# Attention stage of a two-layer metaformer: keys of two heads in one row tile, projections and transposes put into other rounds, LayerNorm statistics behind the reciprocal

## The chip, the cores and the metric

The kernel runs on one core of one Trainium2 chip, as one program in one launch. The metric is the device time in microseconds (us), the median of several runs. Engines are named as in the profile: PE is TensorE's matmul, PEld its weight load, DVE is VectorE, ACT is ScalarE, POOL is GpSimd and SP is the engine that issues most of the DMAs. L604 is line 604 of the kernel before; the change shortens the file, so the same work has a slightly lower number after it (L604 becomes L598, for instance).

## The reference

The reference is a network of two layers on x of shape 8 x 128 x 32 x 32, with a normalisation and a residual around each part. The change touches the first part alone, which is an attention over heads and, for each query row, over the keys of one image row:

```python
xp = jnp.transpose(x, (0, 2, 3, 1))                 # x is already normalised over channels
q = (xp @ wq.T).reshape(b, h, w, n, d)              # n = 8 heads of d = 16
k = (xp @ wk.T).reshape(b, h, w, n, d)
v = (xp @ wv.T).reshape(b, h, w, n, d)
weights = jnp.einsum('bhwnd,bxynd->bnhwxy', q, k) * scale
weights = jax.nn.softmax(weights, axis=-1)          # over y, 32 keys at a time
attn = jnp.einsum('bnhwxy,bxynd->bhwnd', weights, v)
out = attn.reshape(b, h, w, c)
...
x = x + _L0_conv_ref(_ln_c(x), L0_conv_wq, L0_conv_wk, L0_conv_wv)
```

The softmax runs over groups of 32 keys, so each query has 32 separate sums for a head. The rest of the network (a spectral mixer, a deformable convolution, a mixture of experts) is not touched. All arithmetic is in float32.

## The kernel before, in words

A small test at the start decides between a general attention and `attention_bounded`, which leaves out the row maximum; with these inputs the second runs, and the profile shows it from 32 us to about 890 us. Everything below is about it.

**Rounds.** The work is written out by hand as a list of rounds. There are 8 images of 32 rounds each. An image has 8 units of four rounds: a unit is a block of 256 queries (`qc`) and a group of four heads (`hg`). A call `at(round, order, do, ...)` puts a step into a round; the list is sorted by round and by order, and each engine then runs its instructions in that sequence, without overtaking.

**What a round does.** In each round `scores` (L604) computes one PSUM tile of 4 heads x 2 key tiles x 256 queries on PE, in eight matmuls of 32 contraction rows, four side by side in the array. ACT takes the exponential of the tile (L609). The PSUM tile `s` has one buffer of four banks, so the scores of the next round wait until the exponential has read it. POOL adds the two key tiles (`add_tiles`, L618). With a unit starting at round t0, the rest follows later: the sums `z` (L625, PE) in round t0+5, the reciprocals (L632, DVE) behind them, `spread_out` (L639, PE) in t0+6, `divide` (L646, DVE) in t0+6 to t0+9, and `values` (L656, PE) in t0+8 to t0+11. Since every t0 is a multiple of four, PE's regular work depends on the round modulo 4: in round 0 the values of one and a half tiles, in round 1 half a tile and `z`, in round 2 a tile and `spread_out`, in round 3 a tile. Every eight rounds, in round 0 modulo 8, `results` (L673) brings a finished block back to rows of tokens by a matmul with the 0/1 matrix `pick`, ACT copies it, and POOL adds it to the residual (L681).

**What an image needs beside its rounds.** Before its first round an image must be loaded and transposed to tokens (`tokens`, L539), normalised (`layer_norm_pieces`, L79 to L105), transposed back (`channels`, L547, into the tile `hk`), and projected: `keys` (L573), `queries` (L559) and `key_values` (L585). All of these share one PSUM bank, `small_bank`, with `z` and `results`; ACT empties it. The normalisation is 25 pieces: eight statistics on DVE (two instructions each, L79 and L80), nine pieces of an inverse square root by Newton steps on POOL (17 instructions of 128 x 8 elements, L87 to L99), and eight `norm` pieces on ACT (L105), which read the last result `nm` of the POOL pieces. The rounds in which all this stands are lists relative to `first`, the image's first round:

```python
project_at = [first + n for n in (-13, -12, -9, -5, -4, -1, 3, 4, 7, 11)]
turn = {"channels": (first - 20, first - 17)}
...
turn.update(load=first - 42, tokens=(first - 38, first - 34))
norm_at = [first - n for n in (
    37, 36, 35, 34, 33, 32, 32, 31, *range(31, 22, -1), 22, 22, 22, 21, 19, 19, 18, 18
)]
```

**Keys and queries.** Heads of 16 channels are padded to row tiles of 32. Head group `hg` has heads 4 hg to 4 hg + 3, one in each row tile, with zeros in the upper 16 rows of both `wq` and `wk`; so an image has four projections of keys (two head groups x two halves), four of queries and two of values.

Of the kernel before, what the change touches and what calls it, by code (L numbers as in the profile page):

```python
# [399 lines left out]
class BoundedAttention:  # L400
# [6 lines left out]
    def __init__(self, nc, cp):  # L407
        self.nc = nc
        HG, NH = self.HG, self.NH
        self.xc = cp.tile([P, T], F32, name="xc")  # L410
        self.ht = cp.tile([P, NT, C], F32, name="ht")
        self.hk = cp.tile([P, T], F32, name="hk")
        self.wq, self.wk = (cp.tile([P, HG, NH, 32], F32, name=n) for n in ("wq", "wk"))
        self.wv = cp.tile([C, C], F32, name="wv")
        self.group = cp.tile([P, NG], F32, name="group")
        self.spread = cp.tile([P, 2, P], F32, name="spread")
        self.pick = cp.tile([P, HG, NH, HD], F32, name="pick")

    def keys_view(self):
        return self.hk.rearrange("c (r p) -> c r p", p=P)  # L420

    def tokens(self, x, ident, pool, ps):

        nc = self.nc
        nc.sync.dma_start(self.xc, x[0].rearrange("c h w -> c (h w)"))
        xv = self.xc.rearrange("c (i p two) -> c two i p", two=2, p=P)
        st = pool.tile([P, NT, 6], F32, name="f_st")
        mv = pool.tile([P, NT, 2], F32, name="f_mv")
        banks = []
        for par in range(2):  # L430
            pt = ps.tile([P, 4, P], F32, tag="x", name="p_x")
            for i in range(4):
                nc.tensor.transpose(pt[:, i, :], xv[:, par, i, :], ident)
            banks.append(pt)
            for i in range(4):
                nc.vector.bn_stats(st[:, 4 * par + i, :], pt[:, i, :])
                nc.vector.bn_aggr(mv[:, 4 * par + i, :], st[:, 4 * par + i, :])
        rs = inverse_std(nc, pool, mv[:, :, 1], 1e-6, nc.vector)
        for par in range(2):
            for i in range(4):  # L440
                n = 4 * par + i
                nc.vector.tensor_scalar(
                    self.ht[:, n, :], banks[par][:, i, :], mv[:, n, 0:1], rs[:, n : n + 1],
                    ALU.subtract, ALU.mult,
                )
# [3 lines left out]
            nc.scalar.copy(  # L449
                self.keys_view()[:, 4 * par : 4 * par + 4, :].rearrange(  # L450
                    "c r (g m) -> c r g m", m=4
                ),
                pb.rearrange("c i p -> c (i p)").rearrange("c (g r m) -> c r g m", r=4, m=4),
            )

    def matrices(self, wqT, wkT, wvT):
        nc, HG, NH = self.nc, self.HG, self.NH
        for w, src in ((self.wk, wkT), (self.wq, wqT)):
            nc.gpsimd.memset(w, 0.0)
            for hg in range(HG):  # L460
                nc.sync.dma_start(
                    w[:, hg, :, 0:HD],
                    src[:, hg * NH * HD : (hg + 1) * NH * HD].rearrange("c (h d) -> c h d", d=HD),
                )
        nc.sync.dma_start(self.wv, wvT)

        group = self.group
        nc.gpsimd.memset(group, 1.0)
        nc.gpsimd.affine_select(
            out=group, in_=group, pattern=[[-4, NG]], base=0, channel_multiplier=1,  # L470
            compare_op=ALU.is_ge, fill=0.0,
        )
        nc.gpsimd.affine_select(
            out=group, in_=group, pattern=[[4, NG]], base=3, channel_multiplier=-1,
            compare_op=ALU.is_ge, fill=0.0,
        )

# [9 lines left out]
        nc.gpsimd.memset(self.pick, 0.0)  # L487
        for hg in range(HG):
            nc.gpsimd.affine_select(
                out=self.pick[:, hg], in_=self.pick[:, hg], pattern=[[-32, NH], [-1, HD]],  # L490
                base=-HD * hg, channel_multiplier=1, compare_op=ALU.not_equal, fill=1.0,
            )


def attention_bounded(ctx, tc, ident, x, x1d, given, weigh, head):


# [8 lines left out]
    QU = 256  # L506
    QC = T // QU
    UNITS = HG * QC
    wq, wk, wv = given.wq, given.wk, given.wv
    group, spread, pick = given.group, given.spread, given.pick  # L510
    hk = given.keys_view()
# [31 lines left out]
    def channels(par):  # L543
# [6 lines left out]
        nc.scalar.copy(  # L550
            hk[:, 4 * par : 4 * par + 4, :].rearrange("c r (g m) -> c r g m", m=4),
            pt.rearrange("c (g r m) -> c r g m", r=4, m=4),
        )

    def queries(img, hg, par):
# [3 lines left out]
        nc.tensor.matmul(  # L559
            pq, wq[:, hg].rearrange("c h d -> c (h d)"),  # L560
            hk[:, 4 * par : 4 * par + 4, :].rearrange("c r p -> c (r p)"),
            start=True, stop=True,
        )
        nc.scalar.copy(
# [1 line left out]
            pq.rearrange("p (r g m) -> p r g m", r=4, m=4),  # L566
        )

    def keys(img, hg, par):
        if "k" not in img:  # L570
            img["k"] = sb.tile([P, HG, NT, P], F32, tag="k", name="k")
        pk = small_bank("pk")
        nc.tensor.matmul(  # L573
            pk, wk[:, hg].rearrange("c h d -> c (h d)"),
            hk[:, 4 * par : 4 * par + 4, :].rearrange("c r p -> c (r p)"),
            start=True, stop=True,
        )
        nc.scalar.copy(
            img["k"][:, hg, 4 * par : 4 * par + 4, :].rearrange("p c n -> p (c n)"), pk
        )  # L580

    def key_values(b, img, par):
        pv = small_bank("pv")
        for r in range(4):
            nc.tensor.matmul(  # L585
                pv[:, r * P : (r + 1) * P], hk[:, 4 * par + r, :], wv,
                start=True, stop=True,
            )
        img["v"] = vts[b % 2]
# [6 lines left out]
    def scores(img, un, r):  # L596
# [4 lines left out]
        for c in range(2):  # L601
            for j in range(NH):
                rows = slice(32 * j, 32 * j + 32)
                nc.tensor.matmul(  # L604
                    s[:, j, c, :], img["k"][rows, hg, 2 * r + c, :],
                    q[rows, qc * QU : (qc + 1) * QU], start=True, stop=True,
                )
        e = ep.tile([P, NH, 2, QU], F32, tag="e", name="e")
# [59 lines left out]
    def results(b, img, qc, qrt):  # L668
# [1 line left out]
            img["at"] = sb.tile([P, NT, C], F32, tag="at", name="at", bufs=1)  # L670
        po = small_bank("po")
        for i in range(2):
            nc.tensor.matmul(  # L673
                po[:, i * P : (i + 1) * P], qrt["o"][:, i * P : (i + 1) * P],
                pick.rearrange("p g j d -> p (g j d)"), start=True, stop=True,
            )
        nc.scalar.copy(
            img["at"][:, 2 * qc : 2 * qc + 2, :].rearrange("p i c -> p (i c)"), po[:, 0 : 2 * P]
# [16 lines left out]
    for b in range(B):  # L695
        img = {}
        first = 4 * UNITS * b
        project = [
            (keys, img, 0, 0), (keys, img, 0, 1), (queries, img, 0, 0),
            (keys, img, 1, 0), (keys, img, 1, 1), (queries, img, 1, 0),  # L700
            (key_values, b, img, 0), (key_values, b, img, 1),
            (queries, img, 0, 1), (queries, img, 1, 1),
        ]
        if b == 0:
            turn = {"tokens": (0, 0)}
            project_at = (-1, -1, -1, 0, 1, 2, 3, 4, 7, 11)
        else:
            project_at = [first + n for n in (-13, -12, -9, -5, -4, -1, 3, 4, 7, 11)]
            turn = {"channels": (first - 20, first - 17)}
            if b == 1:  # L710
                turn.update(load=0, tokens=(2, 3))
                norm_at = (3, 3, 4, 4, 5, 5, 6, 6) + (6, 7, 7, 8, 8, 8, 9, 9, 9) + (
                    10, 10, 10, 11, 13, 13, 14, 14)
            else:
                turn.update(load=first - 42, tokens=(first - 38, first - 34))
                norm_at = [first - n for n in (
                    37, 36, 35, 34, 33, 32, 32, 31, *range(31, 22, -1), 22, 22, 22, 21, 19, 19, 18, 18
                )]
        if b:
            at(turn["load"], 6, load, b)  # L720
            spread_rounds(
                layer_norm_pieces(nc, sb, lambda i=img: i["xt"], lambda: given.ht, 1e-6), norm_at
            )
            for par in range(2):
                at(turn["channels"][par], 5.5, channels, par)
# [1514 lines left out]
```

## Time and profile before

| | |
|---|---|
| time before, median of 3 runs | 1884.89 us (1883.53 to 1887.96) |
| span of the profiled execution | 1884.7 us |
| that execution's own time | 1886.46 us |
| mean granted clock of PE | 0.959 |
| first and last exponential (L609) | 32.26 us, 886.86 us |
| an image of 32 rounds, images 1 to 5 | 106.6 us |

The profiled execution's own time is 1.8 us above its span, and 1.6 us above the median. A round is best read from the starts of the exponentials: one stands in each round, and the difference of two starts is a round's length. Counting the first exponential as round 0, round r of image b is the exponential number 32 b + r.

### The profile page before, as it was taken

Reading aid. Unit: us, or ns where it says so; the run is one execution under the profiler, and the core shown is the slowest. Engines: PE = TensorE matmul, PEld = TensorE weight load, DVE = VectorE, ACT = ScalarE, POOL = GpSimd, SP = SyncE. Lnnn points to the kernel's source line nnn. Section 1 sums busy time; section 2 is a strip of 40 time slices with the busy share of each in tenths; the row PEclk is TensorE's granted clock in tenths of the full one; section 3 lists DMA queues with packets and bytes.
Section 4 is the critical chain, followed back from the end, with each engine's and each line's share of the span. In section 5 each row is a group of like instructions: output and inputs, shape, how many; then the busy total and the mean of one; then the engine's idle time right before and its main releaser. Section 6 shows DMA issues by size and latency. Waiting matters only on the chain.

```text
span 1884.7 us, 51873 instructions
## 1 busy us (share of the span) xinstructions
PE 1682.4 (89%) x22324; PEld 1033.1 (55%) x22324; DVE 1389.0 (74%) x2107; ACT 1064.8 (56%) x1692; POOL 1157.9 (61%) x1219
## 2 busy tenths in 40 slices
PE   6899999999999999998577899999888497888788
PEld 3455555555555555554233688888665264555555
DVE  3688787878888888888544666666148888999883
ACT  3666666676766667666234455555145655666630
POOL 3778777777878777787221244345126768888740
PEclk9999999999999999999788999999899687999999
DMA  1000000000000000000658322122568775755620
GB/s 30 13 2 24 2 2 24 2 24 2 24 2 24 2 2 24 2 13 2 143 142 242 129 71 71 48 71 59 179 194 263 237 213 153 234 174 164 205 81 21
DMA packets 157998, 156.15 MB, mean 83 GB/s; under 512 B 15424, under 2 KB 136864, under 8 KB 156352
## 3 DMA queue, kind: packets, MB, share of 16 engines
q1 hardware_dynamic: 142400, 102.41, 19.1%
q0 software_dynamic: 15360, 50.34, 8.5%
q8 instruction: 176, 2.88, 0.6%
q14 instruction: 62, 0.51, 0.1%
HBM read 96.39 MB, written 56.33 MB: 81 GB/s over the span
## 4 chain that ended last, share of the span: by engine, by line
PE 60%; DVE 16%; issue 7%; POOL 6%; ACT 4%; DMA 2%; SPq 2%; DVEq 0%; ACTq 0%; POOLq 0%
PE s L604 14%; PE av L656 13%; PE p_g L1958 6%; PE z L625 6%; PE p_z L2007 5%; PE rb L639 4%; PE p_out L1420 3%; DVE ga L1410 3%; DVE g L1317 2%; ACT e L609 2%; PE pq L559 2%; PE pk L573 2%; POOL g L1295 1%; DVE zs L2019 1%; PE po L673 1%
## 5 line engine op out<-in xcount | busy, mean ns | idle before, releaser
L618 POOL TENSOR_TENSOR t<-e 128x1024 f32<-128x1024 f32 x256 | 608.2, 2376 | 204.7 <-ACT e L609 204.4
L646 DVE TENSOR_TENSOR e<-e,rb 128x2048 f32<-128x2048 f32 x256 | 570.4, 2278 | 84.5 <-PE rb L639 84.5
L609 ACT ACTIVATE e<-s 128x2048 f32<-128x2048 f32 x256 | 481.0, 1879 | 255.1 <-PE s L604 252.0
L604 PE MATMUL s<-q,k 32*128 32x256 f32 x4096 | 295.2, 402 | 14.6 <-ACT e L609 13.8
L656 PE MATMUL av<-e,vt 128*32 128x256 f32 x4096 | 287.4, 388 | 4.8 <-DVE e L646 3.5
L1295 POOL DMA_INDIRECT g<-tab,idx x192 | 200.3, 1043 | 134.1 <-ACT cn_m L1515 66.8
L604 PEld LDWEIGHTS s<-q,k 32*128 32x128 f32 x4096 | 185.9, 185 | 137.8 <-ACT e L609 116.9
L1302 ACT ACTIVATE g<-g,w 128x128 f32<-128x128 f32 x604 | 186.4, 390 | 57.0 <-DMA g<-tab,idx 43.2
L1983 POOL TENSOR_SCALAR at<-uc 128x256 f32<-128x256 f32 (+2 forms) x62 | 75.4, 1219 | 173.4 <-PE p_z L2007 128.9
L656 PEld LDWEIGHTS av<-e,vt 128*32 128x32 f32 x4096 | 101.1, 109 | 141.5 <-issue 83.8
L1958 PE MATMUL p_g<-v,a 32*128 32x128 f32 x4096 | 159.3, 284 | 9.4 <-ACT ga L1690 3.7
L632 DVE RECIPROCAL r<-z 128x256 f32<-128x256 f32 x64 | 112.5, 1758 | 70.4 <-PE z L625 70.2
L1958 PEld LDWEIGHTS p_g<-v,a 32*128 32x128 f32 x4096 | 132.3, 186 | 38.3 <-issue 23.0
L1420 PE MATMUL p_out<-ga,ew 128*128 128x512 f32 x256 | 127.5, 645 | 15.5 <-DVE ga L1410 15.4
L625 PE MATMUL z<-t,group 128*32 128x256 f32 x2048 | 122.2, 379 | 0.0
L1692 DVE COPY gb<-p_g 128x512 f32<-128x512 f32 x128 | 82.4, 685 | 46.7 <-PE p_g L1958 46.1
L1692 DVE COPY ga<-p_g 128x512 f32<-128x512 f32 x128 | 82.4, 686 | 44.0 <-PE p_g L1958 44.0
L1690 ACT COPY gb<-p_g 128x512 f32<-128x512 f32 x128 | 68.7, 589 | 69.6 <-PE p_g L1958 68.8
L1690 ACT COPY ga<-p_g 128x512 f32<-128x512 f32 x128 | 68.7, 589 | 66.7 <-PE p_g L1958 66.7
L1410 DVE TENSOR_TENSOR ga<-p_g,tc 128x2048 f32<-128x2048 f32 x32 | 73.0, 2282 | 29.5 <-PE p_g L1401 29.5
L1420 PEld LDWEIGHTS p_out<-ga,ew 128*128 128x128 f32 x256 | 50.1, 205 | 75.6 <-issue 56.2
L625 PEld LDWEIGHTS z<-t,group 128*32 128x32 f32 x2048 | 66.4, 110 | 44.1 <-issue 0.3
(312 smaller groups left out, 2421.3 us busy)
## 6 DMA issues: line engine op xcount, KB each, us to landing
tab<-hx SPq DMA_DIRECT2D x24, 512.0 KB, 5.8
tab<-hx SPq DMA_DIRECT2D x72, 128.0 KB, 5.3
ud<-us SPq DMA_DIRECT2D x8, 1024.0 KB, 5.3
uc<-ud SPq DMA_DIRECT2D x16, 512.0 KB, 4.0
yd<-zs SPq DMA_DIRECT2D x32, 256.0 KB, 3.2
ga<-yd SPq DMA_DIRECT2D x32, 256.0 KB, 3.8
xc<-in_x SPq DMA_DIRECT2D x8, 512.0 KB, 3.9
x1d<-xt SPq DMA_DIRECT2D x8, 512.0 KB, 2.9
```

Of the source, the lines that this page charges most:

```text
L604: nc.tensor.matmul(s[:, j, c, :], img["k"][rows, hg, 2 * r + c, :], q[rows, qc * QU : (qc + 1) * QU], start=True, stop=True,)
L609: nc.scalar.activation(e.rearrange("p j c q -> p (j c q)"), s.rearrange("p j c q -> p (j c q)"), AF.Exp, scale=float(HD) ** -0.5,)
L618: nc.gpsimd.tensor_add(t, e[:, :, 0, :], e[:, :, 1, :])
L625: nc.tensor.matmul(un["z"][32 * j : 32 * j + 32, 0:QU], group, un["t", r][:, j, :], start=(r == 0), stop=(r == 3), skip_group_check=True,)
L646: nc.vector.tensor_tensor(e, e, un["rb"].unsqueeze(2).to_broadcast([P, NH, 2, QU]), ALU.mult)
L656: nc.tensor.matmul(qrt["av"][32 * j : 32 * j + 32, 0:QU], img["v"][:, 2 * r + c, P * hg + 32 * j : P * hg + 32 * j + 32], un["e", r][:, j, ...
L1295: nc.gpsimd.indirect_dma_start(out=t["g", i][:, tap].rearrange("p k c -> p (k c)"), out_offset=None, in_=rows, in_offset=bass.IndirectOffs ...
L1302: nc.scalar.activation(t["g", i][:, tap, k, :], t["g", i][:, tap, k, :], AF.Identity, scale=t["w"][:, i, tap, k : k + 1],)
L1420: nc.tensor.matmul(t["out"], self.ew[:, first + e, :], xg[:, e, :], start=(first + e == 0), stop=(first + e == NE - 1), skip_group_check=True,
L1690: self.nc.scalar.copy(dst, src)
L1692: self.nc.vector.tensor_copy(dst, src)
L1958: nc.tensor.matmul(banks[j][:, i * P : (i + 1) * P], self.a[rows, 4 * n + i, :], self.v[rows, ch].rearrange("p f k -> p (f k)"), start=Tru ...
```

## The change

It makes four edits, all in the attention.

- **Keys of two heads in one row tile.** Row tile j now holds heads 2 j and 2 j + 1 in the order of the channels. `wk` is the plain 128 x 128 matrix, one projection gives the keys of all heads, and an image has two key projections in the place of four. `wq` keeps one head of each pair and zeros for the other, for each `hg`. `wv` is permuted so that the values come out in channel order, and `results` becomes two transposes in the place of two matmuls with `pick`.
- **Projections one a round, in rounds 3 modulo 4**: -13, -9, -5, -1, 3, 7, 11, 15.
- **Turns in rounds 4, 12, 20, 28**: the transposes of `tokens` and `channels`. Since image b is still read when image b+1 is written, `hk` gets a second buffer.
- **Statistics behind the reciprocal ("inversion")**: the DVE statistics stand in rounds -35, -31 and -27, which are rounds 1 modulo 4; the nine POOL pieces are then in four rounds (two, two, two and three), and the ACT pieces in rounds -22 to -14. Images 0 and 1, which start during the first image, have lists of their own.

```diff
-        self.hk = cp.tile([P, T], F32, name="hk")
-        self.wq, self.wk = (cp.tile([P, HG, NH, 32], F32, name=n) for n in ("wq", "wk"))
-        self.wv = cp.tile([C, C], F32, name="wv")
+        self.hk = [cp.tile([P, T], F32, name=f"hk{n}") for n in range(2)]
+        self.wq = cp.tile([P, HG, NH, 32], F32, name="wq")
+        self.wk = cp.tile([C, C], F32, name="wk")
+        self.wv = cp.tile([C, HG, NH, HD], F32, name="wv")
...
+        nc.sync.dma_start(self.wk, wkT)
+        nc.gpsimd.memset(self.wq, 0.0)
+        for hg in range(HG):
+            at = slice(HD * hg, HD * hg + HD)
+            nc.sync.dma_start(
+                self.wq[:, hg, :, at], wqT.rearrange("c (h n) -> c h n", n=2 * HD)[:, :, at]
+            )
+            nc.sync.dma_start(
+                self.wv[:, hg], wvT.rearrange("c (h n) -> c h n", n=2 * HD)[:, :, at]
+            )
...
-    def keys(img, hg, par):
+    def keys(b, img, par):
         if "k" not in img:
-            img["k"] = sb.tile([P, HG, NT, P], F32, tag="k", name="k")
+            img["k"] = sb.tile([P, NT, P], F32, tag="k", name="k")
...
-                    s[:, j, c, :], img["k"][rows, hg, 2 * r + c, :],
+                    s[:, j, c, :], img["k"][rows, 2 * r + c, :],
...
-            nc.tensor.matmul(
-                po[:, i * P : (i + 1) * P], qrt["o"][:, i * P : (i + 1) * P],
-                pick.rearrange("p g j d -> p (g j d)"), start=True, stop=True,
+            nc.tensor.transpose(
+                po[:, i * P : (i + 1) * P], qrt["o"][:, i * P : (i + 1) * P], ident
             )
...
         project = [
-            (keys, img, 0, 0), (keys, img, 0, 1), (queries, img, 0, 0),
-            (keys, img, 1, 0), (keys, img, 1, 1), (queries, img, 1, 0),
+            (keys, b, img, 0), (keys, b, img, 1), (queries, b, img, 0, 0), (queries, b, img, 1, 0),
             (key_values, b, img, 0), (key_values, b, img, 1),
-            (queries, img, 0, 1), (queries, img, 1, 1),
+            (queries, b, img, 0, 1), (queries, b, img, 1, 1),
         ]
+        project_at = [first + n for n in (-13, -9, -5, -1, 3, 7, 11, 15)]
         if b == 0:
             turn = {"tokens": (0, 0)}
-            project_at = (-1, -1, -1, 0, 1, 2, 3, 4, 7, 11)
+            project_at = (-1, -1, -1, 3, 4, 7, 11, 15)
+        elif b == 1:
+            turn = {"load": 0, "tokens": (8, 12), "channels": (18, 20)}
+            norm_at = (9, 9, 10, 10, 13, 13, 14, 14) + (14, 14, 15, 15, 15, 15, 16, 16, 16) + (
+                17, 17, 17, 17, 18, 18, 19, 19)
         else:
-            project_at = [first + n for n in (-13, -12, -9, -5, -4, -1, 3, 4, 7, 11)]
-            turn = {"channels": (first - 20, first - 17)}
-            if b == 1:
-                turn.update(load=0, tokens=(2, 3))
-                norm_at = (3, 3, 4, 4, 5, 5, 6, 6) + (6, 7, 7, 8, 8, 8, 9, 9, 9) + (
-                    10, 10, 10, 11, 13, 13, 14, 14)
-            else:
-                turn.update(load=first - 42, tokens=(first - 38, first - 34))
-                norm_at = [first - n for n in (
-                    37, 36, 35, 34, 33, 32, 32, 31, *range(31, 22, -1), 22, 22, 22, 21, 19, 19, 18, 18
-                )]
+            turn = {
+                "load": first - 42, "tokens": (first - 36, first - 28),
+                "channels": (first - 20, first - 12),
+            }
+            norm_at = [first - n for n in (35, 35, 31, 31, 27, 27, 27, 27)] + [
+                first - n for n in (26, 26, 25, 25, 24, 24, 23, 23, 23)
+            ] + [first - n for n in (22, 22, 21, 21, 19, 18, 15, 14)]
```

More of the change, by code (lines that the diff above doesn't have):

```diff
@@ L411, in __init__, with keys_view @@
         self.ht = cp.tile([P, NT, C], F32, name="ht")
-        self.hk = cp.tile([P, T], F32, name="hk")
-        self.wq, self.wk = (cp.tile([P, HG, NH, 32], F32, name=n) for n in ("wq", "wk"))
-        self.wv = cp.tile([C, C], F32, name="wv")
+        self.hk = [cp.tile([P, T], F32, name=f"hk{n}") for n in range(2)]
+        self.wq = cp.tile([P, HG, NH, 32], F32, name="wq")
+        self.wk = cp.tile([C, C], F32, name="wk")
+        self.wv = cp.tile([C, HG, NH, HD], F32, name="wv")
         self.group = cp.tile([P, NG], F32, name="group")
         self.spread = cp.tile([P, 2, P], F32, name="spread")
-        self.pick = cp.tile([P, HG, NH, HD], F32, name="pick")
-    def keys_view(self):
-        return self.hk.rearrange("c (r p) -> c r p", p=P)
+    def keys_view(self, b):
+        return self.hk[b % 2].rearrange("c (r p) -> c r p", p=P)
     def tokens(self, x, ident, pool, ps):
@@ L449, in tokens @@
             nc.scalar.copy(
-                self.keys_view()[:, 4 * par : 4 * par + 4, :].rearrange(
+                self.keys_view(0)[:, 4 * par : 4 * par + 4, :].rearrange(
                     "c r (g m) -> c r g m", m=4
@@ L457, in matrices @@
         nc, HG, NH = self.nc, self.HG, self.NH
[L458 to L465, printed above, removed]
+        nc.sync.dma_start(self.wk, wkT)
[8 more added lines that the diff above has]
+            )
         group = self.group
@@ L484, in matrices @@
             )
[L487 to L492, printed above, removed]
 def attention_bounded(ctx, tc, ident, x, x1d, given, weigh, head):
@@ L508, in attention_bounded @@
     UNITS = HG * QC
-    wq, wk, wv = given.wq, given.wk, given.wv
-    group, spread, pick = given.group, given.spread, given.pick
-    hk = given.keys_view()
+    wq, wk, wv = given.wq, given.wk, given.wv.rearrange("c g j d -> c (g j d)")
+    group, spread = given.group, given.spread
     cp = ctx.enter_context(tc.tile_pool(name="a_const", bufs=1))
@@ L541, in tokens, with channels @@
         nc.scalar.copy(xt.rearrange("p a c -> p (a c)"), pt)
-    def channels(par):
+    def channels(b, par):
         pt = small_bank("pb")
@@ L550, in channels, with queries @@
         nc.scalar.copy(
-            hk[:, 4 * par : 4 * par + 4, :].rearrange("c r (g m) -> c r g m", m=4),
+            given.keys_view(b)[:, 4 * par : 4 * par + 4, :].rearrange(
+                "c r (g m) -> c r g m", m=4
+            ),
             pt.rearrange("c (g r m) -> c r g m", r=4, m=4),
         )
-    def queries(img, hg, par):
+    def queries(b, img, hg, par):
         if "q" not in img:
@@ L560, in queries @@
             pq, wq[:, hg].rearrange("c h d -> c (h d)"),
-            hk[:, 4 * par : 4 * par + 4, :].rearrange("c r p -> c (r p)"),
+            given.keys_view(b)[:, 4 * par : 4 * par + 4, :].rearrange("c r p -> c (r p)"),
             start=True, stop=True,
@@ L567, in queries @@
         )
-    def keys(img, hg, par):
+    def keys(b, img, par):
         if "k" not in img:
-            img["k"] = sb.tile([P, HG, NT, P], F32, tag="k", name="k")
+            img["k"] = sb.tile([P, NT, P], F32, tag="k", name="k")
         pk = small_bank("pk")
         nc.tensor.matmul(
-            pk, wk[:, hg].rearrange("c h d -> c (h d)"),
-            hk[:, 4 * par : 4 * par + 4, :].rearrange("c r p -> c (r p)"),
+            pk, wk, given.keys_view(b)[:, 4 * par : 4 * par + 4, :].rearrange("c r p -> c (r p)"),
             start=True, stop=True,
@@ L578, in keys @@
         nc.scalar.copy(
-            img["k"][:, hg, 4 * par : 4 * par + 4, :].rearrange("p c n -> p (c n)"), pk
+            img["k"][:, 4 * par : 4 * par + 4, :].rearrange("p c n -> p (c n)"), pk
         )
@@ L585, in key_values @@
             nc.tensor.matmul(
-                pv[:, r * P : (r + 1) * P], hk[:, 4 * par + r, :], wv,
+                pv[:, r * P : (r + 1) * P], given.keys_view(b)[:, 4 * par + r, :], wv,
                 start=True, stop=True,
@@ L724, in attention_bounded @@
             for par in range(2):
-                at(turn["channels"][par], 5.5, channels, par)
+                at(turn["channels"][par], 5.5, channels, b, par)
         for par in range(2):
```

## The prediction, written before the changed kernel had run

> **What bounds the kernel now.** I read the page first, engines and then the chain of waits by line.
>
> ```profile
> PE 1682.4 (89%) x22324; PEld 1033.1 (55%) x22324; DVE 1389.0 (74%) x2107; ACT 1064.8 (56%) x1692; POOL 1157.9 (61%) x1219
> ...
> PE s L604 14%; PE av L656 13%; PE p_g L1958 6%; PE z L625 6%; PE p_z L2007 5%; PE rb L639 4%; PE p_out L1420 3%; DVE ga L1410 3%; DVE g L1317 2%; ACT e L609 2%; PE pq L559 2%; PE pk L573 2%; POOL g L1295 1%; DVE zs L2019 1%; PE po L673 1%
> ```
>
> PE carries the end, and the attention lines are much of it. But an average does not say which rounds PE bounds. So the timeline of PE from round 30 of image 3 to round 0 of image 4 (start, duration):
>
> ```profile
> 459.18 1.15 PE L604 MATMUL s<-q,k 32*128 32x256 f32 x16
> 460.25 1.07 PE L656 MATMUL av<-e,vt 128*32 128x256 f32 x16
> 461.25 1.13 PE L639 MATMUL rb<-r,spread 64*128 64x256 f32 x8
> 462.32 0.74 PE L539 MATMUL pt<-ident,xc 128*128 128x128 f32 x4
> 462.99 1.15 PE L604 MATMUL s<-q,k 32*128 32x256 f32 x16
> 464.07 1.07 PE L656 MATMUL av<-e,vt 128*32 128x256 f32 x16
> 465.07 1.13 PE L559 MATMUL pq<-hk,wq 128*128 128x512 f32 x2
> 466.19 1.15 PE L604 MATMUL s<-q,k 32*128 32x256 f32 x16
> ...
> 468.26 0.71 PE L673 MATMUL po<-pick,o 128*128 128x128 f32 x4
> ```
>
> Start to start, s costs PE 1.07 us, av 1.00, rb 1.07, a pt turn 0.67, a projection 1.06 to 1.12. Round 30 (2 modulo 4, with a turn) is 462.99 - 459.18 = 3.81 long: PE without a gap. Round 31 (3 modulo 4, with a projection) is 3.20. The floor is the loop through the single s tile: s to the exponential's start 1.24, exponential 1.88, back to s 0.05: 3.17. A round costs the larger of 3.17 and PE's sum. The differences of the exponentials' starts, meaned over images 1 to 5, agree (rounds 0 to 31, four a line):
>
> ```
>  0: 3.31 3.37 3.20 3.18     16: 3.28 3.37 3.17 3.17
>  4: 3.73 3.37 3.16 3.16     20: 3.71 3.36 3.19 3.19
>  8: 3.29 3.38 3.17 3.17     24: 3.29 3.36 3.81 3.16
> 12: 3.24 3.40 3.21 3.19     28: 3.70 3.37 3.82 3.17
> ```
>
> Rounds over the floor: 1 modulo 4 (z, untouched); 4, 20, 28 with a projection beside one and a half tiles of values; 26 and 30 with a turn beside rb; 0, 8, 16, 24 with results. A projection in 3 modulo 4 is free: 1.07 + 1.00 + 1.06 = 3.13.
>
> The second thing is who else stands in ACT's queue ahead of the exponential. Timelines of POOL and of ACT, in the first image:
>
> ```profile
> 72.41 2.37 POOL L618 TENSOR_TENSOR t<-e 128x1024 f32<-128x1024 f32 x1
> ...
> 75.91 0.25 POOL L99 TENSOR_SCALAR lp_nm<-lp_nm 128x8 f32<-128x8 f32 x1
> ```
>
> ```profile
> 72.44 1.88 ACT L609 ACTIVATE e<-s 128x2048 f32<-128x2048 f32 x1 [1.49 <-PE s L604]
> 76.19 1.26 ACT L105 ACTIVATE ht<-xt,lp_nm,lp_y 128x128 f32<-128x128 f32 x3 [1.87 <-POOL lp_nm L99]
> 77.36 1.85 ACT L609 ACTIVATE e<-s 128x2048 f32<-128x2048 f32 x1
> ```
>
> Here POOL's inversion was late, ACT waited 1.87 us in a norm piece, and the exponential behind it came 4.92 us after the last. Later POOL has one inversion piece a round and is just in time: in image 3, L99 ends at 395.25 and the norms start at 395.70.
>
> **The change part by part.** All against the profiled execution (span 1884.70, own time 1886.46, which is 1.6 above the median).
>
> *Projections.* Leave rounds 4, 20, 28; one is added in round 15, where it is free. *Turns.* Leave rounds 26, 30 and 17; come into 4, 12, 20, 28. A pb turn in round 12 today gives 3.24. A pt turn is 0.07 dearer (L539 325 ns against L547 286 ns a transpose): 1.00 + 0.67 + 0.57 + 1.07 = 3.31, say 3.30. So round 4: 3.73 to 3.30, -0.43; 28: -0.40; 20: 3.71 to 3.24, -0.47; 26 and 30: 3.81 and 3.82 to 3.17, -1.29.
>
> *Results by transpose.* The row near it is pt: four transposes are four PE instructions and 0.67, so two are 0.33, against 0.65 for po today. (Upper end: 0.65, no gain.) PE's sum falls to 2.97, under the floor: rounds 0, 8, 16, 24 together -0.49.
>
> *Keys in one row tile.* The score matmuls keep count and shape, so L604 stays. Two key copies of 0.59 leave ACT an image; it has room in those rounds: nothing. DMAs: five for the weights as before, on SP at 3 to 7 us; the first projection starts at 21.8 behind hk. The wk memset leaves POOL at 1.9, 14 us ahead of need: nothing. If the cover were gone, at most 0.3.
>
> *Second hk.* It only removes a wait that ends in time now: nothing.
>
> *Statistics on DVE.* Two pairs of 0.45 between reciprocal and divide fit into DVE's wait of 1.41 for rb. In round 5 there are four: 1.80, so the divides start 0.4 late; DVE then has 0.95 idle before the next reciprocal, and values come 1.9 after their divide: nothing. Were that gone, 0.4 an image.
>
> *Inversion on POOL: the new wait.* Nine pieces (17 instructions) now stand in rounds 6 to 9, four, four, four and five instructions behind each round's t, with the residual add in round 8. From the POOL rows: 17 instructions took 0.61 + 1.00 + 1.61 + 1.39 = 4.61 at 64.5 to 76.1; a t followed at once takes 2.34; the add 0.69. From the t of round 6: 4 x 2.34 + 4.61 + 0.69 = 14.66 us until nm is there. Exponential 10 ends 3 x 3.17 + 3.37 = 12.88 after exponential 6, and that t starts 0.08 after it: 12.80. So nm is 1.9 late. Behind the norms stand, on ACT, the exponential of round 11, and behind that PE's next scores. Two norms take 0.86 of the 1.29 between exponentials (0.1 overlaps): spare 0.5. Delay 1.4 an image, for images 2 to 7. (Lower end 0, if POOL keeps up; upper 1.9, no spare.) In round 11 a query copy and two norms, 0.5 + 0.9, overfill the 1.29: +0.1. z takes the t of round 7, which is only 0.3 late, against 1.8 of room.
>
> Image 1 is worse. Its statistics end behind the divide of round 14, at 5.3 after that exponential's start; then 4 instructions (1.1), t 2.34, 8 (2.2), t 2.34, add 0.69, 5 (1.4): nm at 15.4. Four norms of 1.7 end at 17.2. Exponential 18 is due at 3 x 3.17 + 3.37 = 12.9: delay 4.3. (Lower end 1.75, what round 10 lost today with three norms; upper 5.)
>
> *Start of image 0.* Rounds 0 to 5 take 27.3 now. Keys leave round 0 behind two turns: 8.40 to 5.64. Keys, queries and turns leave rounds 1 and 2. Here a rule decides: the windows view, and s, which lasts 2.09 at 38.47 but 1.15 at 42.58:
>
> ```profile
> 35.60:39.02 3.42, 2.75 (x7) 1.02 (x10) 0.00 (x0) 1.03 (x2) 0.96 (x1) 1.00 0.44 153
> 39.02:42.43 3.41, 3.41 (x18) 1.20 (x10) 0.00 (x0) 1.92 (x2) 0.00 (x0) 1.00 0.00 0
> ```
>
> (The second number is PE's busy time; the PEclk column has no record this early.) PE stayed at half speed through windows 80% busy and was released by the first full one. The Trainium skill (TensorE: Matmul & The Clock Gate, Part 1: The HAM clock gate) calls the warm-up about 3.4 us of time, and says not to count its ramp. By that, PE is fast by round 1 as now, and rounds 0 to 5 come to 22.2: -5.1. By the trace, the removed matmuls were what filled the window: s then alternates with the exponential, half busy, until the projections of rounds 3 and 4: rounds of 5.6, 4.1, 4.1, 4.8, 3.2 to 4.1, 3.2: about 25.8, -1.5. I take the trace.
>
> *PE's idle during the new waits.* The same page (Why this matters for your kernels) has it that idle gaps under about 3 us keep the clock. The trace:
>
> ```profile
> 76.56:79.98 3.42, 1.73 (x14) 0.88 (x18) 3.42 (x3) 3.42 (x6) 2.62 (x2) 1.00 0.00 0
> ...
> 899.17:902.58 3.41, 1.39 (x24) 0.66 (x28) 3.41 (x3) 0.00 (x0) 0.00 (x0) 1.00 0.01 2
> 902.58:906.00 3.42, 2.89 (x32) 0.87 (x24) 3.42 (x2) 0.00 (x0) 0.00 (x0) 0.50 0.00 0
> ```
>
> 1.73 busy of 3.42 kept the full clock, 1.39 lost it for the next window, with no gap over 1.5. The delay of 1.4 leaves about 2.0 busy: nothing. In the 4.3 of image 1 a window falls below 1.4: by the rule (idle 2.6) nothing, by the trace a half-speed window, +1.5. I take 1.5.
>
> **Sum.** Images 1 to 5: -0.43 - 0.40 - 0.47 - 1.29 - 0.49 = -3.08, +1.5 for the waits, = -1.58 each, -7.9. Image 6 (no turns in 26 and 30 today, none in 28 after): -1.92 + 1.5 = -0.4. Image 7 (no successor): -0.52 - 0.56 = -1.1. Image 0: start -1.5; round 10 to the floor -1.75; rounds 20, 24, 26, 28, 30 together -2.3; small ones in 8, 12, 16, 18 +0.3; wait +4.3; clock +1.5: +0.6. Together -8.8: span 1875.9, own time 1877.7; from the median, 1876.1. Nothing behind the attention changes in order, so it moves along.
>
> **The rivals.**
>
> *POOL keeps up* (no norm waits). POOL is idle 205 us today ahead of L618. Against it: the adds above, and the row at 76.19. Then the waits and the clock term, 6 x 1.5 + 4.3 + 1.5 = 14.8, fall away: 1861.3.
>
> *The clock falls in every norm wait* (slower). Each wait leaves PE idle just after busy rounds; if the window's busy time is under a point between 1.39 and 1.73, a half-speed window or two follow, 1.7 us each with PE the bound. Two in each of six images: -8.8 + 6 x 3.4 = +11.6: 1896.5. With one it is +1.4, no change. It decides from a wait of about 2.0, against my 1.4. For it: the 4.3 wait. Against: 1.73 held.
>
> *POOL's lateness reaches z as well,* another 1 us an image: -8.8 + 7 = about -2, no change: 1883. For it: t of rounds 8 to 10 is up to 2 us late. Against: z of round 13 needs t of round 11, by which the ACT wait has let POOL catch up. Into this I also count that moved turns cost what they saved.
>
> **How the numbers follow.** Forecast 0.74, POOL keeps up 0.10, clock 0.08, no gain 0.08. A measurement tells about 0.2%, 3.8 us. Faster by more: 0.74 + 0.10 = 0.84; within: 0.08; slower: 0.08. The forecast's own range is 1871 to 1881 (wait 0.7 to 2.0 an image, start -5 to +1). The range goes to 1863 and 1883, which leaves out most of the first rival and the second.
>
> **What would show it.** Right: rounds 4, 28 at 3.3, 20 at 3.24, 26 and 30 at 3.17, 0 modulo 8 at 3.17; norms waiting for lp_nm in round 10 (round 10 about 4.6 long) and in round 17 (7.7); L604 at 2.09 until about 52 us. Wrong: no wait of L105 on POOL; PEclk 0.50 between 60 and 880 us; L625 waiting for L618; rounds 4, 20, 28 still at 3.7.

## The result and the profile after

The changed kernel takes 1877.35 us (median of 20 runs, 1867.93 to 1885.53), against 1885.44 us for the kernel before in its own 20 runs (1881.84 to 1892.32). The ratio is 0.9955, 95% interval 0.9943 to 0.9967: faster by about 0.45%. The prediction was 1876.1, from a change of -8.8 us; the medians differ by 8.1. The single runs of the changed kernel spread over 17.6 us, more than the forecast's range of 1871 to 1881, so a hit within 1.3 us says little by itself. What the forecast is worth is read below from the rounds.

The page of the changed kernel's profiled execution (1878.91 us, span 1877.2), engines and then the chain of waits by line:

```profile
PE 1673.7 (89%) x22228; PEld 1024.7 (55%) x22228; DVE 1385.4 (74%) x2107; ACT 1052.6 (56%) x1676; POOL 1156.8 (62%) x1215
...
PE s L598 13%; PE av L650 9%; PE p_g L1951 6%; PE z L619 5%; PE p_z L2000 5%; ACT e L603 5%; PE rb L633 3%; PE p_out L1413 3%; DVE ga L1403 3%; POOL t L612 2%; DVE g L1310 2%; DMA g<-tab,idx 2%; PE pq L554 2%; PE p_mix L1245 1%; DVE e L640 1%
```

PE lost 8.7 us of busy time, and its share of the span stayed. What tells more is the chain's line: the exponential (`e`, L603) and POOL's `t` (L612) now carry part of the chain. The loop through the s tile and a wait on POOL would look like this; the rounds have to show it.

The round lengths, from the starts of the exponentials in the two profiles (means over images 1 to 5 where nothing else is said):

| | before | predicted | after |
|---|---|---|---|
| rounds 26 and 30 (turn left) | 3.81, 3.82 | 3.17 | 3.17, 3.16 |
| round 20 (projection left, turn in) | 3.71 | 3.24 | 3.24 |
| rounds 4 and 28 (the same) | 3.73, 3.70 | 3.30 | 3.32, 3.32 |
| rounds 0, 8, 16, 24 together (transposes) | 13.17 | 12.68 | 12.70 |
| round 10 (norms behind POOL) | 3.17 | 4.6 | 4.62 |
| all 32 rounds | 106.63 | 105.05 | 105.04 |
| image 0, rounds 0 to 5 | 27.33 | 25.8 | 25.00 |
| image 0, round 17 | 3.37 | 7.7 | 7.36 |
| image 0, rounds 18 and 19 | 6.34 | 6.6 at most, +1.5 for the clock | 8.69 |
| image 0, all 32 rounds | 115.36 | 116.0 | 115.62 |
| first to last exponential | 854.6 | 845.8 | 845.7 |

PE's timeline of the changed kernel, round 28 of image 3 and round 0 of image 4:

```profile
448.61 1.15 PE L598 MATMUL s<-q,k 32*128 32x256 f32 x16
449.69 1.07 PE L650 MATMUL av<-e,vt 128*32 128x256 f32 x16
450.69 0.74 PE L532 MATMUL pt<-ident,xc 128*128 128x128 f32 x4
451.36 0.64 PE L650 MATMUL av<-e,vt 128*32 128x256 f32 x8
451.93 1.15 PE L598 MATMUL s<-q,k 32*128 32x256 f32 x16
...
461.64 1.15 PE L598 MATMUL s<-q,k 32*128 32x256 f32 x16
462.72 1.07 PE L650 MATMUL av<-e,vt 128*32 128x256 f32 x16
463.72 0.44 PE L667 MATMUL po<-ident,o 128*128 128x128 f32 x2
464.09 0.64 PE L650 MATMUL av<-e,vt 128*32 128x256 f32 x8
464.81 1.15 PE L598 MATMUL s<-q,k 32*128 32x256 f32 x16
```

From s to s, the first is 3.32 (PE full), the second 3.17: after the last values PE is done at 464.73 and waits for the exponential.

One line of the lists of waits bears on the forecast (total, times, longest; the kernel before, then the changed one):

```profile
ACT ht L105 <- POOL lp_nm L99: 1.9, 1, 1.9
```

```profile
ACT ht L105 <- POOL lp_nm L99: 15.7, 7, 3.9
```

One of the seven waits is image 1's, 3.93; the other six are 1.93 to 1.99. POOL and then ACT in image 3 show how one comes about:

```profile
379.50 2.38 POOL L612 TENSOR_TENSOR t<-e 128x1024 f32<-128x1024 f32 x1 [1.00 <-ACT e L603]
...
388.67 0.73 POOL L674 TENSOR_TENSOR xt<-xt,at 128x256 f32<-128x256 f32 x1
...
390.40 2.37 POOL L612 TENSOR_TENSOR t<-e 128x1024 f32<-128x1024 f32 x1
...
393.90 0.24 POOL L99 TENSOR_SCALAR lp_nm<-lp_nm 128x8 f32<-128x8 f32 x1
```

```profile
390.34 1.88 ACT L603 ACTIVATE e<-s 128x2048 f32<-128x2048 f32 x1 [1.46 <-PE s L598]
394.17 0.88 ACT L105 ACTIVATE ht<-xt,lp_nm,lp_y 128x128 f32<-128x128 f32 x2 [1.96 <-POOL lp_nm L99]
394.96 1.85 ACT L603 ACTIVATE e<-s 128x2048 f32<-128x2048 f32 x1
```

From the t of round 6 (379.50) to the end of L99 (394.14) it is 14.64 us; the sum in the prediction said 14.66. The exponential of round 11 stands behind the two norms and comes 4.62 after the last.

And the windows view at the wait of image 1 (stretch and its length; busy time of PE, PEld, DVE, ACT and POOL; granted clock; the rest is DMA):

```profile
97.00:100.41 3.41, 2.23 (x16) 1.21 (x12) 2.19 (x1) 1.84 (x5) 3.07 (x7) 1.00 0.03 7
100.41:103.82 3.41, 2.04 (x17) 1.22 (x16) 3.41 (x3) 2.82 (x4) 2.22 (x2) 0.50 0.00 0
103.82:107.24 3.42, 3.42 (x22) 1.10 (x18) 3.28 (x2) 2.64 (x3) 1.67 (x2) 0.50 0.00 0
```

The granted clock fell from 1.00 to 0.50 for two windows, and the s of round 19 took 2.09 instead of 1.15.

### The profile page after: what moved, and what is told of

It reads as the page before. It is cut to its first block, busy times and chain, and to the rows that moved or that the text cites. A ratio compares the mean times of both kernels' runs of the same rounds, so it can differ in the third digit from the quotient of the medians.

```text
span 1877.2 us, 51680 instructions
## 1 busy us (share of the span) xinstructions
PE 1673.7 (89%) x22228; PEld 1024.7 (55%) x22228; DVE 1385.4 (74%) x2107; ACT 1052.6 (56%) x1676; POOL 1156.8 (62%) x1215
## 4 chain that ended last, share of the span: by engine, by line
PE 55%; DVE 15%; POOL 9%; ACT 8%; issue 8%; DMA 4%; SPq 2%; DVEq 0%; POOLq 0%; ACTq 0%
PE s L598 13%; PE av L650 9%; PE p_g L1951 6%; PE z L619 5%; PE p_z L2000 5%; ACT e L603 5%; PE rb L633 3%; PE p_out L1413 3%; DVE ga L1403 3%; POOL t L612 2%; DVE g L1310 2%; DMA g<-tab,idx 2%; PE pq L554 2%; PE p_mix L1245 1%; DVE e L640 1%
## 5 line engine op out<-in xcount | busy, mean ns | idle before, releaser
L612 POOL TENSOR_TENSOR t<-e 128x1024 f32<-128x1024 f32 x256 | 608.4, 2377 | 192.4 <-ACT e L603 190.2
L603 ACT ACTIVATE e<-s 128x2048 f32<-128x2048 f32 x256 | 481.0, 1879 | 261.5 <-PE s L598 254.3
L598 PE MATMUL s<-q,k 32*128 32x256 f32 x4096 | 299.0, 406 | 25.4 <-ACT e L603 21.2
```

The lines of the kernel that those rows point to most:

```text
L598: nc.tensor.matmul(s[:, j, c, :], img["k"][rows, 2 * r + c, :], q[rows, qc * QU : (qc + 1) * QU], start=True, stop=True,)
L603: nc.scalar.activation(e.rearrange("p j c q -> p (j c q)"), s.rearrange("p j c q -> p (j c q)"), AF.Exp, scale=float(HD) ** -0.5,)
L612: nc.gpsimd.tensor_add(t, e[:, :, 0, :], e[:, :, 1, :])
```

## The experiments

The theory: a round costs the larger of the 3.17 loop and PE's sum, so the moved and removed work gives 3.08 us an image; and the norm pieces on ACT, which wait for POOL's inversion, take half of it back and most of image 0's gain. The rivals: the late round 10 has another cause; moved turns, not fewer keys, carry the gain; the clock falls at any such wait. Eight kernels were run. The first four were timed against the kernel before on one chip (1886.12 us there), the second four on another (1933.25 us there). The attention takes the same time on both (images 1 to 5 of the kernel with both alterations below take 103.72 us each on the first, and with the fill, which touches the start alone, 103.72 on the second) and the rest of the program differs, so I compare ratios, or the time from the first to the last exponential in the profiles, "attention" below: 854.6 before, 845.7 changed.

**Take the wait of images 2 to 7 away.** The POOL pieces move ahead by up to two rounds, nothing else:

```diff
-                first - n for n in (26, 26, 25, 25, 24, 24, 23, 23, 23)
+                first - n for n in (26, 26, 26, 26, 25, 25, 25, 25, 25)
```

> The changed kernel with one list altered: for images 2 to 7 the nine inversion pieces stand in rounds 6 and 7 (four and five) in the place of 6 to 9 (two, two, two, three). Theory (the norm pieces on ACT wait for nm because two t, one residual add and the inversion stand ahead of it on POOL): nm is then there after one t fewer than two, about 9.3 us behind the t of round 6, before the norms want it at 12.8; round 10 falls from 4.62 to 3.17 in images 1 to 6 of the rounds, no wait of L105 on L99 there, 6 x 1.45 = 8.7 us less than the changed kernel: about 1868.6. t of round 7 is 2.2 late against 3.3 of room before z of round 9, so 3.37 stays for round 9. Rival (ACT is late in round 10 for another reason, such as its own load or a busy POOL port): round 10 stays at 4.6 and the time at 1877. Second rival (z now waits for the late t of round 7): round 9 rises from 3.37 by up to 1.2, and half or more of the gain is given back: about 1873 to 1876.

Measured: 1870.45 us, ratio to before 0.9914 (0.9896 to 0.9932); attention 836.6, 9.1 less than the changed kernel. Round 10 is 3.22 in all six images, round 9 stays at 3.37. ACT's timeline at the same place of image 3:

```profile
386.73 1.88 ACT L603 ACTIVATE e<-s 128x2048 f32<-128x2048 f32 x1 [1.47 <-PE s L598]
388.50 0.87 ACT L105 ACTIVATE ht<-xt,lp_nm,lp_y 128x128 f32<-128x128 f32 x2
389.95 1.88 ACT L603 ACTIVATE e<-s 128x2048 f32<-128x2048 f32 x1 [0.58 <-ACT ht L105]
```

The norms follow the exponential at once. So the wait was POOL's order of work, not its amount: the same 17 instructions now have two t fewer ahead of them, and the residual add behind them. (nm is there 9.5 us after the t of round 6 in image 3, from 375.89 to 385.40, for 14.64 before.) Images 1 to 6 gave 8.2; the other 0.9 is that the clock fell for one window here in image 0, not for two.

**Take image 1's wait away.** Its tokens, statistics and inversion move into the early rounds, in which POOL and DVE have little else:

```diff
-            turn = {"load": 0, "tokens": (8, 12), "channels": (18, 20)}
-            norm_at = (9, 9, 10, 10, 13, 13, 14, 14) + (14, 14, 15, 15, 15, 15, 16, 16, 16) + (
-                17, 17, 17, 17, 18, 18, 19, 19)
+            turn = {"load": 0, "tokens": (2, 6), "channels": (18, 20)}
+            norm_at = (3, 3, 4, 4, 9, 9, 9, 9) + (10, 10, 10, 11, 11, 11, 12, 12, 12) + (
+                14, 14, 14, 16, 17, 17, 17, 18)
```

> The changed kernel with only image 1's lists altered: its turns of tokens in rounds 2 and 6 in the place of 8 and 12, its statistics in 3, 4 and 9, the inversion in 10 to 12 and the norm pieces in 14 to 18; the channels stay in 18 and 20. Theory (the 7.36 of round 17 is the wait for image 1's nm, and 4.08 and 4.61 of rounds 18 and 19 are the half clock that PE's idle brought): round 17 comes to 3.4, 18 to 3.7 (a turn beside rb), 19 to 3.2, no granted clock of 0.5 between 55 and 880 us, rounds 8 and 12 at 3.17: 4.0 + 0.4 + 1.4 + 0.25 = 6.0 us less than the changed kernel, about 1871.3. Rival (the clock falls there for another reason, as at about 100 us of any run): round 17 is short but 0.5 stays for two windows: 4.3 less, about 1873.

Measured: 1871.18 us, ratio 0.9913 (0.9890 to 0.9936); attention 839.9, 5.8 less than the changed kernel. Round 17 is 3.32, 18 is 3.73, 19 is 3.14, and no clock of 0.5 stands between 52 and 880 us. So the two slow rounds went with the wait. That they were the clock and not the wait itself shows in two profiles in which the wait stands: in the first experiment the clock fell for one window, and round 18 took 3.14 and round 19 4.70; with only the turns of tokens back (below) it held, and both took 3.15 or less.

**Both together.** No further edit.

> Both alterations of the two kernels before it together, which should beat the kernel before and the changed one. Theory: the two add, 8.7 + 6.0 = 14.7 us less than the changed kernel: about 1862.6; no image round over 3.45 from round 20 on, except those with a turn of tokens at 3.32. Rival (another engine becomes the bound when the waits are gone, DVE at 2.8 us a round or POOL with its t): the gains do not add, 1866 or more.

Measured: 1865.35 us (1861.29 to 1866.82), ratio 0.9891 (0.9873 to 0.9910). Attention in the profile 827.8, 17.9 less than the changed kernel; but 4.4 of it is not the edit's: rounds 0 to 3 took 14.27 where the kernel with image 1's wait away, whose first rounds are the same, took 18.62: the clock was released at 33.6 us and not at 51.5. Without that it is 13.6. The sum of the two is 8.2 + 5.8 = 14.0, since the first one's other 0.9 is a part of the second one's gain; round 10 of image 3 is 3.50 here and not 3.22, which is most of the rest. The medians differ by 12.0 from the changed kernel, less than the 14.7 that were expected. No wait of L105 on POOL is left.

**Keys in one row tile alone,** in the schedule of the kernel before:

```diff
-        project_at = [first + n for n in (-13, -9, -5, -1, 3, 7, 11, 15)]
+        project_at = [first + n for n in (-13, -9, -5, -1, 3, 4, 7, 11)]
...
+            norm_at = [first - n for n in (
+                37, 36, 35, 34, 33, 32, 32, 31, *range(31, 22, -1), 22, 22, 22, 21, 19, 19, 18, 18
+            )]
```

(and the turns of the kernel before, image 1's lists too; image 0's last projections stand in rounds 2, 3, 4, 7 and 11.)

> The keys of two heads in one row tile alone (with the permuted values and results by transpose), in the schedule of the kernel before: turns in -38, -34, -20, -17, its lists of statistics and inversion, projections in -13, -9, -5, -1, 3, 4, 7, 11. Theory (a round costs the larger of 3.17 and PE's sum): rounds 20 and 28 lose their projection, 3.71 and 3.70 to 3.17, results rounds 3.29 to 3.17: -1.56 in each of images 1 to 6, -0.5 in image 7, -1.3 in image 0, and the start (keys out of rounds 0 and 1, but a half clock for longer) about 0: 11 us less than the kernel before, about 1874.5, so two or three less than the changed kernel, whose moved turns then cost more than they bring. Rival (the schedule carries the gain and fewer keys are hidden anyway): 4 us less than before at most, 1881 or more.

Measured: 1875.46 us, ratio 0.9946 (0.9928 to 0.9964); attention 845.5, against 845.7 for the whole change. Images 1 to 5 take 105.08, against 105.04. Rounds 20 and 28 are 3.17. PE's timeline shows round 28 empty of a projection:

```profile
449.74 1.50 PE L650 MATMUL av<-e,vt 128*32 128x256 f32 x24
451.83 1.15 PE L598 MATMUL s<-q,k 32*128 32x256 f32 x16 [0.59 <-ACT e L603]
```

So the smaller part of the change, two key projections fewer and results by transpose, is worth all that the whole change brings; what the new rounds give, the new wait takes. Without that wait (the first experiment) images 1 to 5 take 103.66, so the new rounds alone are worth 1.42 an image. (The start was expected to cost nothing and is slower: rounds 0 to 5 took 29.0, against 25.0 with the whole change and 27.3 before, most of it at half clock with image 1's turns in rounds 2 and 3.)

**Only the turns of tokens back,** with the old lists of the normalisation, for images 2 to 7:

```diff
-                "load": first - 42, "tokens": (first - 36, first - 28),
+                "load": first - 42, "tokens": (first - 38, first - 34),
```

> The changed kernel with, for images 2 to 7, the turns of tokens back in rounds -38 and -34 and the lists of statistics, inversion and norms of the kernel before; projections, channels, keys and image 1 as changed. Theory (what the moved turns bring is lost again in the norms' wait): rounds 26 and 30 go from 3.17 to 3.82, +1.29 an image; rounds 4 and 28 from 3.32 to 3.17, -0.30; round 10 from 4.62 to 3.17, -1.45: -0.46 in each of images 1 to 5, together about -3: 1875, no change that can be told from the changed kernel. Rival (the turns' move is worth having, and the wait comes from their later rounds only in small part): 1 us an image or more slower, 1884.

Measured: 1916.16 us, ratio 0.9927 (0.9903 to 0.9950), attention 838.5. Rounds 26 and 30 are 3.79 and 3.82, rounds 4 and 28 3.17, round 10 3.17: images 1 to 5 take 104.59, 0.45 less than with the whole change, as expected. The ratio is lower than expected all the same. Of the 7.2 us less in attention, these five images are 2.2 and image 6, whose rounds 26 and 30 carry no turn, is 1.6. The other 3.5 are image 0's (clock released at 33.0 us, and no fall behind round 17), in which this kernel does not differ before round 26, so they are no gain of the edit. Seen so, the moved turns of tokens are worth 1.0 an image and cost 1.45.

**A longer wait,** to see when the clock falls: four or nine more POOL instructions of 128 x 8 ahead of nm.

```diff
+        if n == 7:
+            for _ in range(more):                # 4 for images 2 to 4, 9 for 5 to 7
+                nc.gpsimd.tensor_mul(w, y, y)
```

> The changed kernel with extra POOL instructions of 128 x 8 ahead of the last inversion step: four for images 2 to 4, nine for images 5 to 7. Theory (PE's idle costs only itself until a 3.41 us window has under about 1.4 us of PE work): round 10 goes from 4.62 to 5.7 with four and 7.1 with nine; with four, PE idles about 2.6 in one piece, and the clock falls only where that piece lies within one window; with nine, 4.0, it falls always, and rounds 11 and 12 then rise from 3.2 to 4 or more. Together +11 for the waits and 5 to 10 for the clock. Rival (the clock needs an idle of over 3.4 us, a whole window): no fall with four, a fall in some only with nine. Second rival (any wait of this kind makes it fall): a fall in all six.

Measured, in one profiled run: round 10 is 5.47, 5.47 and 5.50 with four and 6.90 with nine. PE idles for about 2.25 us in one piece with four and 3.67 with nine. The clock fell behind one of the three shorter waits and behind all three longer ones. Windows view of this kernel, two waits with four (the first without a fall) and one with nine:

```profile
289.95:293.37 3.42, 1.62 (x28) 1.09 (x32) 3.42 (x3) 3.31 (x5) 3.00 (x2) 1.00 0.00 0
293.37:296.78 3.41, 3.41 (x56) 1.79 (x52) 2.01 (x1) 2.57 (x3) 2.56 (x2) 1.00 0.02 5
395.77:399.18 3.41, 1.51 (x24) 1.01 (x28) 3.41 (x3) 3.32 (x6) 2.99 (x2) 1.00 0.00 0
399.18:402.59 3.41, 3.41 (x28) 1.44 (x24) 2.10 (x1) 2.24 (x2) 2.57 (x2) 0.50 0.00 0
501.58:504.99 3.41, 1.21 (x6) 0.30 (x2) 3.41 (x3) 1.21 (x3) 2.86 (x10) 1.00 0.01 2
504.99:508.40 3.41, 1.93 (x16) 1.22 (x16) 3.41 (x2) 2.68 (x4) 2.99 (x2) 0.50 0.00 0
```

The window with 1.62 of PE work kept the clock, the one with 1.51 lost it. An equal wait falls on either side, by where it lies in the grid of windows. A fall cost 1.6 us in image 3 (107.44 against 105.88 for the two without), and an estimated 1.6 to 2.4 with nine, where 107.3 would stand without one (105.88, and 1.42 for the longer round 10). The changed kernel's six steady waits leave 2.01 to 2.67 in their emptiest windows, and the clock fell behind none.

**Results by matmul again,** with the identity:

```diff
-            nc.tensor.transpose(
-                po[:, i * P : (i + 1) * P], qrt["o"][:, i * P : (i + 1) * P], ident
-            )
+            nc.tensor.matmul(
+                po[:, i * P : (i + 1) * P], qrt["o"][:, i * P : (i + 1) * P], ident,
+                start=True, stop=True,
+            )
```

> The changed kernel with results by two matmuls with the identity in the place of two transposes. Theory (PE's sum is the round): four PE instructions and 0.65 us instead of two and 0.37, rounds 0, 8, 16 and 24 at 3.29 instead of 3.17, +0.45 an image, about 4 us in all. Rival (the transpose form is no cheaper, the rounds are short for lack of other work): no difference.

PE's timeline in round 0 of image 4 shows four PE instructions for the two that the transposes took:

```profile
462.90 0.71 PE L667 MATMUL po<-ident,o 128*128 128x128 f32 x4
```

Measured, in one profiled run: the four rounds are 3.27, 3.30, 3.29 and 3.28, as expected. But the image costs 0.28 more, not 0.45: round 10 fell from 4.62 to 4.45. That fits a longer round 8, which gives POOL more time ahead of the norms: what is saved in front of a wait that another engine ends makes that wait longer.

**Both alterations and filled pauses at the start.** Five matmuls without a reader fill PE's pauses before round 2:

```diff
+    def fill(n):
+        pf = rp.tile([P, 512], F32, tag="av", name="pf")
+        nc.tensor.matmul(
+            pf[:, 0:n], wk, given.keys_view(0)[:, 0:4, :].rearrange("c r p -> c (r p)")[:, 0:n],
+            start=True, stop=True,
+        )
...
+            if b == 0:
+                at(par, 5.5, fill, (256, 512)[par])
...
+            if b == 0 and n < 3:
+                at(when, 6, fill, 128)
```

> Both alterations (inversion in rounds 6 and 7, image 1 early) and five matmuls of 128 to 512 columns into an idle PSUM bank, with no reader, which fill PE's pauses of 0.7 to 2 us between the first projection and the scores of round 2. Theory (the half clock ends with the first of the free-running 3.41 us windows that PE fills to about 85% or more, and which window that is depends on their phase): PE is busy without a pause over 0.7 from 21.8, so it is released by 28.7 in every run; the first exponential comes at 30.3 instead of 32.2, rounds 0 to 3 take 4.3, 3.1, 3.2, 3.7 as they happened to in the profile of both alterations without fill: about 2 us less than that profile, 6 less than a run whose release comes at 52; median about 1861. Rival (the release is a matter of time since the first matmuls, or matmuls without a reader don't count): 1865 and the release where it was, each fill adding its own 0.1 to 1 us.

Measured: 1901.44 us, ratio to before 0.9844 (0.9820 to 0.9867), the lowest ratio of the study. The clock was released at 30.7 us, the first exponential came at 31.27 and rounds 0 to 3 took 4.32, 3.14, 3.17, 3.64. PE's timeline:

```profile
26.66 2.08 PE L554 MATMUL pq<-hk,wq 128*128 128x512 f32 x2 [0.25 <-ACT k L572]
28.53 0.64 PE L681 MATMUL pf<-hk,wk 128*128 128x128 f32 x2
29.42 1.75 PE L598 MATMUL s<-q,k 32*128 32x256 f32 x16 [0.25 <-ACT q L559]
31.09 0.75 PE L532 MATMUL pt<-ident,xc 128*128 128x128 f32 x4
```

The s of round 0 changes speed in its middle. The release came a window later than expected (23.9 to 27.3 was busy for 3.11 and did not do). The gain is not shown. Against the profile without the fill, which took the same rounds 0 to 3, the first exponential is 0.88 us earlier and the attention as long (827.8). That the release is earlier in every run one profile cannot show. The ratio is lower by 0.0047, some 9 us, more than the 2 to 6 expected, and it was timed on the other chip, where the kernel without the fill was not.

## Why the prediction was right, point by point

**What bounds a round** held throughout: the larger of 3.17 and PE's sum gave each moved item to 0.02 us, and the image to 0.01. The two terms for the turns of tokens and for results were read from pt and po rows that stood in other rounds; that was near enough (two transposes of results took 0.37, from 463.72 to 464.09, for 0.33).

**The wait on POOL** was the step that mattered, and it was found by adding up instructions that no row showed together. The wait of the kernel before in image 0 gave both the price of each piece and the proof that the queue behaves so. The delay was 1.45 an image for 1.4. Round 11's 0.1 was 0.04.

**Image 1's wait** was 4.0 for 4.3: L105 waited 3.93 us, and the four norms took 1.65.

**The clock behind it** was mis-sized: 2.3 us for 1.5, since the half clock held for two windows. Whether it falls, and for how long, is luck. Four of the other kernels keep image 1's lists and wait as long (round 17 is 7.21 to 7.39). In three of them the clock fell for one window. With only the turns of tokens back it did not fall, and rounds 18 and 19 took 3.15 and 3.14. So the wait itself costs round 17 alone. Windows view of that kernel, and then of the one with the early inversion, where it fell:

```profile
94.46:97.88 3.42, 2.27 (x19) 1.10 (x11) 2.01 (x2) 1.59 (x5) 3.08 (x7) 1.00 0.01 2
97.88:101.29 3.41, 1.92 (x28) 1.16 (x30) 3.41 (x3) 3.37 (x6) 2.22 (x2) 1.00 0.02 5
101.29:104.70 3.41, 3.41 (x46) 1.56 (x38) 3.41 (x2) 3.38 (x5) 2.63 (x2) 1.00 0.00 0
```

```profile
99.93:103.34 3.41, 1.92 (x26) 1.10 (x30) 3.41 (x3) 3.37 (x6) 2.21 (x2) 1.00 0.02 5
103.34:106.76 3.42, 3.42 (x22) 0.89 (x14) 3.42 (x2) 2.53 (x3) 2.63 (x2) 0.50 0.00 0
```

The clock can fall though PE never idles for 3 us, which is the limit that the Trainium skill gives (TensorE: Matmul & The Clock Gate, Why this matters for your kernels): PE's idle in the changed kernel was in pieces of 1.0 and 1.4 us. There the prediction was right to follow the trace. But the trace's limit (1.39 busy loses it) was read too coarsely: 1.92 kept the clock in one window and lost it in another, and the window 97.00:100.41 counts 2.23 and lost it. Of those 2.23, 1.12 is one turn of four transposes stretched over 1.54 us between the norms that feed it, and without it the window has 1.11. The Trainium skill (TensorE: Matmul & The Clock Gate, Part 4: PE-mode transpose) says that transposes don't count as busy in the same way. Here they counted at least in part. The window 94.46:97.88 above has 0.93 of such transposes and 1.33 of other work and kept the clock, where 1.51 without any lost it (the longer wait); and a turn without a pause helped to release the clock (the last section). So the stretching is the likelier reason; no run tests it.

**The start** was -2.3 for -1.5. The rounds came as listed (5.65, 4.09, 4.11, 4.77, 3.19, 3.20); I had put round 4 between its two cases, and it took the fast one. The release went from 42.4 to 52.6 us when matmuls were taken out, where by the time budget of the Trainium skill (TensorE: Matmul & The Clock Gate, Part 1: The HAM clock gate) PE would have been fast by round 1. But this, too, is one draw for each kernel. In the five profiles with these first rounds the release came at 52.6, 52.1, 47.7, 47.6 and 33.0 us (there with a second fall from 39.9 to 50.1), and rounds 0 to 5 took 25.0, 25.0, 24.0, 24.0 and 22.7. The last is near the 22.2 that the budget gave.

**Image 7** gave 0.8 for 1.1: its round 10 is 3.35, not 3.17. There DVE works without a pause from 802.18 us to the end of the reciprocal at 811.29, with statistics of the network's next part (L79, L80) between its divides, and rb on PE starts only at 811.35, some 0.2 after the values were through. The forecast had not looked at DVE there.

**Behind the attention** the span moved by 1.4 less than the attention (997.9 us there before, 999.3 after). The four profiles of the first chip, with the same code there, range from 995.5 to 1005.0, so I take nothing from this.

**The rivals.** POOL did not keep up. The clock did not fall in the six steady waits. z did not wait for a late t: round 13 is 3.32. The forecast's own wait, though, was close to the clock rival: 0.9 us more of it brought the first fall.

So the images' -3.08 + 1.5 is what the method gave, and it came back in every profile with these rounds (images 1 to 5 take 105.04, and 105.01 with image 1's wait away). Image 0's +0.3 for +0.6 is made of terms that change from run to run.

## What to carry to other kernels

When work is moved out of the bounding engine's full rounds, add up what is queued, instruction by instruction, on the engine that prepares its operands, and see what stands behind the first reader in that reader's queue: here 17 tiny POOL instructions, spread as two a round instead of one, put an exponential 1.45 us late and took back half of the gain. Here the order alone cured it. And test the parts of a change alone: the plain part (fewer projections) was worth all of the net gain, while the clever part paid for its own wait until the inversion was moved ahead by up to two rounds.

## What the runs showed of the hardware that I had not expected

The start depends on luck. In each of the ten profiles PE's clock was released at the end of a 3.41 us window of which PE filled 3.00 us or more. The windows before it, from the first projection on, had 2.83 at most, but for two with 3.10 and 3.11 that did not release it; so the limit is not sharp in the profile's busy times. The windows lie on a grid that is not tied to the program: with the same first rounds, the release came at 51.5 us in one profile and at 33.6 in another, and rounds 0 to 3 took 18.62 and 14.27, 4.35 us apart. PE's timeline and the windows view of the latter (both alterations):

```profile
27.25 2.07 PE L554 MATMUL pq<-hk,wq 128*128 128x512 f32 x2 [0.68 <-ACT k L572]
29.99 2.09 PE L598 MATMUL s<-q,k 32*128 32x256 f32 x16 [0.68 <-ACT q L559]
32.02 1.13 PE L532 MATMUL pt<-ident,xc 128*128 128x128 f32 x4
```

```profile
26.73:30.15 3.42, 2.23 (x6) 0.66 (x6) 1.82 (x11) 1.05 (x2) 0.00 (x0) 1.00 0.00 0
30.15:33.56 3.41, 3.00 (x20) 1.79 (x20) 0.00 (x0) 1.41 (x1) 0.00 (x0) 1.00 0.00 0
```

The second window, busy for 3.00, released it. 1.13 of that is a turn of transposes without a pause. The other 1.87 would not have done: in the kernel before, windows with 2.74 of matmuls alone released nothing.

A fall of the clock had its limit between 1.51 and 1.62 of 3.41 in the six waits of the longer-wait kernel, whose windows hold no transpose. That is no rule for the whole program. Behind the attention, in windows without a transpose as well, 1.74 lost the clock in one kernel (both alterations) and 1.41 kept it in another (results by matmul):

```profile
1040.49:1043.90 3.41, 1.74 (x43) 1.36 (x38) 2.63 (x5) 2.15 (x4) 3.41 (x6) 1.00 0.00 0
1043.90:1047.31 3.41, 2.46 (x36) 1.68 (x40) 1.88 (x4) 0.00 (x0) 2.36 (x3) 0.50 0.05 11
```

```profile
928.35:931.76 3.41, 1.41 (x4) 0.34 (x2) 0.32 (x2) 0.00 (x0) 2.22 (x11) 1.00 0.96 198
931.76:935.18 3.42, 0.00 (x0) 0.00 (x0) 0.00 (x0) 1.53 (x4) 1.36 (x7) 1.00 0.76 133
```

What else decides stays open.
